# Three edits to a two-layer attention kernel: the last image's fourth row tile behind the flag, the projection's first tiles by head pairs, and one addition between normed tiles

## Chip, cores and metric

One NeuronCore of one Trainium2 chip runs the whole kernel. The time is device microseconds of one execution; the runs agree within about 0.3%. Engines are named as in the profile: PE is TensorE (PEld are its weight loads), DVE is VectorE, ACT is ScalarE, POOL is GpSimd, SP is SyncE, which issues DMAs.

## The reference, cut to what matters

The input is 8 images of 1024 tokens (32 x 32) with 384 channels, in float32. Each image goes through two layers.

```python
def _gn(v, G=32, eps=1e-5): ...            # group norm, 32 groups of 12 channels
def _ln_t(v, eps=1e-5): ...                # layer norm over the channels

# layer 0: 6 heads of 64, biases by row and column position
qkv = x.reshape(b, hw, c) @ qkv_w + qkv_b
attn = einsum('bqd,bkd->bqk', q * SCALE, k) + rel_h + rel_w
out = einsum('bqk,bkd->bqd', softmax(attn), v)          # per head
x = x + (out.reshape(b, h, w, c) @ proj_w + proj_b)     # qkv from _gn(x)
# layer 1: one causal head over 1024 tokens, width 384
t = x.reshape(b, 1024, 384)
q, k, v = (_ln_t(t) @ W for W in (Wq, Wk, Wv))
t = t + softmax(where(causal, q @ k.T * scale, -inf)) @ v
# layer 1: two linear maps with signs of weights (384 -> 1536 -> 384), each followed by
# a scaling by the largest absolute value of the image; only images 0 to 4 are not zero here
t = t + bitlinear(gelu(bitlinear(_ln_t(t), W1, b1)), W2, b2)
```

The groups of the last part are single images (8 // 5 = 1), so that images 5, 6 and 7 get nothing from it.

## The kernel before

**Order of images.** Images are done one after the other in `ORDER`: 5, 0, 1, 2, 3, 4, 6, 7. `AFTER` maps each image to the next one; image 7 alone isn't in it. While one image is in layer 1, work for the next one's group norm is slipped in.

**Order of the work.** The program is written in order, and the scheduler of the tile framework places each instruction in its engine's queue, by priority and by its own model of when operands are ready. Two helpers tie it down: `tc.issue_after(ins)` and `behind_of(ins)` put what is issued inside them behind the instruction named. `last_matmul`, `last_product`, `last_ended` and `last_normed` hold the last such instruction of a chain. Engines meet through semaphores. All eight PSUM banks are one pool of 128 x 512 float32 tiles (`o_tile`), so that a new product waits until a bank has been read out.

**Layer 0** (`layer0`, `attend0_fast`). Tokens are halves of 512, heads are pairs of two (`p` = 0, 1, 2). For each pair and half, eight key tiles give scores (L905, L909), ScalarE takes the exponent (L916), the values are summed with them (L931), and VectorE adds up the exponents (L921, L923). `oT` holds the result with channels on partitions, as three blocks of 128 channels, one for each pair. The pair and half before is divided late: its sums go through a small product `den` (L965), a reciprocal (L972), a widening (L979, L980), and a multiplication. For the last pair, half 0 is multiplied by L1013 and half 1 by L1016, both on VectorE. Then the output projection is made for eight tiles of 128 tokens (`project`, L520): three products over the pairs, accumulated in a bank. Tiles 0 to 3 lie in half 0 and are asked for at L1018 in the order tile by tile; tiles 4 to 7 come by `begin`. `more(j)` (L1024) adds a tile to the residual `xt`.

**Layer 1, projections** (`attention1`). `normed` takes mean and variance of four tiles and gives the normed tiles (L490). `turn_normed` transposes each of them (three products with the identity into one bank `pt`, L427; ScalarE copies it out, L428). Queries and values are made with a fast multiplication of 3 x 3 blocks: 15 products instead of 18 (`ProductSet`, in the order `PROD_ORDER`) are summed in six banks A to F. Partial sums are copied out by ScalarE (`keep`, L639) and combined by GpSimd (L659). When a bank's last product and its second operand are there, `final` subtracts or adds the two on VectorE (L1098 for queries, L1106 for values), which ends the bank's use. The tenth product makes the operand `n3`, which completes bank E's second operand `m7`; before, `of_q.final` is None in that step, so that E's addition comes with the next call, behind all four normed tiles of the second half:

```python
of_q.final = None
of_q.run(1)
with behind_of(last_ended[0]), behind_of(of_q.last_copy):
    tiles, _ = next(norm)
    tiles = list(tiles)
last_ended[0] = last_normed[0]
of_q.run(4, put_queries(0))
```

**Layer 1, attention** (`attend1_fast`). `scores(c)` makes the transposed scores of key tile `c`, and `values(j)` sums the products of row tile `j` over its `j + 1` key tiles. The values carry a 385th column of ones, so that the sum of a row stands beside it. VectorE copies that sum (L1205), takes its reciprocal (L1206), and adds the scaled row to `xt` (L1207). `values(c - 2)` follows `scores(c)`; tiles 6 and 7 come last. For images 0 to 4 the feed-forward part follows.

**The end.** `check` (L561, L562) notes the sums and reciprocals in `seen`. After all images, `judge` compares them with limits (L282), reduces them to `worst` (L284, L285), adds that over partitions by a product (L287), and writes `flag` (L288). Every engine loads the flag (L1497) and branches (L1498): if it isn't zero, the whole work is done once more in a safer form, the general path. Here it is zero. The outputs are stored by pairs of row tiles (L1482); for image 7 SyncE does that, in the order (0, 1), (2, 3), (4, 5), (6, 7).

Of the kernel before, what the change touches and what calls it, by code (L numbers as in the profile page):

```python
# [19 lines left out]
P = 128  # L20
B, H, W, C = 8, 32, 32, 384
T = H * W
NJ = T // P
# [68 lines left out]
def conv_attn_hybrid(  # L92
# [182 lines left out]
    seen = const.tile([P, 2, N_SEEN], F32, name="seen")  # L275
    flag = const.tile([1, 1], I32, name="flag")

    def judge(pools):

        bad = pools.page("bad")[:, : 2 * N_SEEN].rearrange("p (i n) -> p i n", i=2)  # L280
        for i, most in enumerate((SUM_MAX, RSUM_MAX)):
            nc.vector.tensor_scalar(bad[:, i, :], seen[:, i, :], most, -1.0, ALU.is_lt, ALU.mult)  # L282
        worst = const.tile([P, 1], F32, name="worst")
        nc.vector.tensor_reduce(worst, bad, AX.XY, ALU.max)  # L284
        nc.vector.tensor_scalar_add(worst, worst, 1.0)  # L285
        ps = pools.o_tile("bad")
        nc.tensor.matmul(ps[0:1, 0:1], worst, ones[:, 0:1], start=True, stop=True)  # L287
        nc.vector.tensor_copy(flag, ps[0:1, 0:1])  # L288

# [125 lines left out]
    def stages(pools):  # L417
# [471 lines left out]
        def attend0_fast(residual, b, q, k, r, v, later):  # L889
# [125 lines left out]
            rb = widened(p, half, reciprocals(*waiting))  # L1015
            nc.vector.tensor_tensor(oT[:, p, t], av, rb, ALU.mult)  # L1016
            with behind_last():
                begun = {j: project(wproj_sb, slice(0, C), oT, j, f"pj_{b}_{j}") for j in range(4)}  # L1018

            def begin(j):  # L1020
                begun[j] = project(wproj_sb, slice(0, C), oT, j, f"pj_{b}_{j}")
# [56 lines left out]
        def attention1(xt, more, b, between, start):  # L1078
# [36 lines left out]
            if pools.fast:  # L1115
                begin, more = more
                for j in range(4):
                    more(j)
                *_, (tiles, _) = normed(xt, 0, f"1_{b}")
                tiles = list(tiles)  # L1120
                begin(4)
                norm = normed(xt, 1, f"1_{b}")
                with behind_of(last_normed[0]):
                    more(4)
                    next(norm)
                last_ended[0] = last_normed[0]
                begin(5)
                turn_normed(xT, 0, tiles)
                begin(6)
                begin(7)  # L1130
                forms = forms_of(0)
                with behind_of(last_ended[0]):
                    for j in range(5, NJ):
                        more(j)
                        next(norm)
                    next(norm)
                last_ended[0] = last_normed[0]
                of_q, of_v = products(0, forms)
                of_q.run(9, put_queries(0))
                of_q.final = None  # L1140
                of_q.run(1)
                with behind_of(last_ended[0]), behind_of(of_q.last_copy):
                    tiles, _ = next(norm)
                    tiles = list(tiles)
                last_ended[0] = last_normed[0]
                of_q.run(4, put_queries(0))
                of_v.run(1)
                of_q.run(1)
                with behind_of(last_product[0]):
                    turn_normed(xT, 1, tiles)  # L1150
                last_product[0] = last_transpose[0]
                forms = forms_of(1)
                of_v0, (of_q, of_v) = of_v, products(1, forms)
                of_v0.run(13, put_values(0))
                of_q.run(1)
                of_v0.run(1)
                of_q.run(13, put_queries(1))
                of_v.run(1)
                of_q.run(1)
                queries_ended[0] = last_ended[0]  # L1160
                of_v.run(14, put_values(1))
            else:
                layer_norm_T(xt, xT, 0, f"1_{b}")
                layer_norm_T(xt, xT, 1, f"1_{b}")
                for m in range(NC):
                    queries(0, m)
                    queries(1, m)
                for j in range(NJ):
                    values(j)
# [6 lines left out]
        def attend1_fast(xt, b, q, xT, v, other, start):  # L1176
# [5 lines left out]
            def scores(c):  # L1182
# [15 lines left out]
                    nc.scalar.activation(pr[:, at : at + 512 - lo], sc[:, lo:], AF.Exp)  # L1198
                return pr

            def values(j):
                av = pools.o_tile(f"av1_{b}_{j}")
                for c in range(j + 1):
                    nc.tensor.matmul(av[:, : C + 1], prs[c][:, ts(j - c, P)], v[:, c, :], start=(c == 0), stop=(c == j))  # L1204
                nc.vector.tensor_copy(tot[:, j : j + 1], av[:, C : C + 1])  # L1205
                nc.vector.reciprocal(rt[:, j : j + 1], tot[:, j : j + 1])  # L1206
                nc.vector.scalar_tensor_tensor(  # L1207
                    xt[:, j, :], av[:, :C], rt[:, j : j + 1], xt[:, j, :], ALU.mult, ALU.add
                )

            prs, masked = [], [None]
            for c in range(NJ):
# [10 lines left out]
                signs.clear()  # L1223
            start()
            values(NJ - 2)
            values(NJ - 1)
            check(tot, rt, b * PER_IMAGE + PER_IMAGE - 1)

        def attend1_general(xt, b, q, xT, v, other, start):
            next(other, None)  # L1230
            mask = pools.work.tile([P, P], F32, tag="mask", name=f"mask_{b}")
            make_causal_mask(nc, mask, mask_val=MASKED)

            def scores(j):
                n = (j + 1) * P
                sc = []
                for half in range((n + 511) // 512):
                    sc.append(pools.o_tile(f"s1_{b}_{j}_{half}"))
                    w = min(512, n - half * 512)
                    for k in range(NC):  # L1240
                        nc.tensor.matmul(
                            sc[half][:, :w], q[:, j // 4, k, ts(j % 4, P)], xT[:, half, k, :w],
                            start=(k == 0), stop=(k == NC - 1),
                        )
                own = sc[j // 4][:, ts(j % 4, P)]
                nc.vector.tensor_tensor(own, own, mask, ALU.add)
                tot = pools.small.tile([P, 1], F32, tag="tot1", name=f"tot1_{b}_{j}")
                return softmax_numerator(sc, n, tot, f"1_{b}_{j}"), tot

            def values(j, got):  # L1250
                pr, tot = got
                prT = transpose_probs(pr, j + 1, f"prT1_{b}_{j}")
                av = pools.o_tile(f"av1_{b}_{j}")
                for c in range(j + 1):
                    nc.tensor.matmul(av[:, :C], prT[:, c, :], v[:, c, :C], start=(c == 0), stop=(c == j))
                rt = pools.small.tile([P, 1], F32, tag="rt1", name=f"rt1_{b}_{j}")
                nc.vector.reciprocal(rt, tot)
                nc.vector.scalar_tensor_tensor(xt[:, j, :], av[:, :C], rt, xt[:, j, :], ALU.mult, ALU.add)

            pipelined(range(NJ), scores, values)  # L1260
# [137 lines left out]
        def run(pools):  # L1398
# [49 lines left out]
            for b in ORDER:  # L1448
# [37 lines left out]
                if b < B_FFN:  # L1486
                    unfinished.append(finish)
                else:
                    finish(*range(NJ))

        run(pools)

    with ExitStack() as scope:
        pools = Pools(scope, tc, "f")
        stages(pools)
        judge(pools)
    failed = nc.values_load(flag[0:1, 0:1], min_val=0, max_val=P)  # L1497
    with tc.If(failed > 0), ExitStack() as scope:  # L1498
        stages(Pools(scope, tc, "g"))
# [38 lines left out]
```

## Time and profile before

| | us |
|---|---|
| median of 3 runs | 2274.53 |
| lowest and highest | 2273.84, 2279.3 |
| profiled execution, its own time | 2274.38 |
| its span, first to last instruction | 2272.6 |
| PE busy | 2258.0 (99%) |
| DVE busy | 1627.1 (72%) |
| ACT busy | 1208.3 (53%) |
| POOL busy | 527.9 (23%) |
| mean granted TensorE clock | 0.999 |

The span is what the trace covers; the execution's own time is 1.8 us longer. A line of the page or of the groups gives a source line, an engine and operation, what is written from what, how often, the busy time and mean ns. In a list of waits, a line names the waiting engine and line, what it waited for, the total us, how often, and the longest. A timeline line gives the start, the length, and in brackets the idle time before it. A "q" behind an engine's name means its queue: register, branch, semaphore and DMA-issuing instructions. Matmuls overlap in the array, and their ends are modelled.

### The profile page before, as it was taken

The numbers are of one execution on the slowest core, as the hardware profiler recorded it, in microseconds if no ns is written. First come the engines' busy times: TensorE is split into PE (matmuls) and PEld (weight loads), VectorE is DVE, ScalarE is ACT, GpSimd is POOL, SyncE is SP. The second block draws the span as 40 slices with busy tenths as digits, with TensorE's granted clock in tenths as the row PEclk, the third lists the DMA queues.
The fourth block names the chain that finished last, engine by engine and source line by source line (L and its number), as shares of the span: only waits on it lengthen the run. The fifth ranks groups of instructions, "written<-read, shape, count | busy, mean of one in ns | idle before, by whom it ended". The sixth has DMA issues, their size and how long they took to land.

```text
span 2272.6 us, 30133 instructions
## 1 busy us (share of the span) xinstructions
PE 2258.0 (99%) x10589; PEld 1384.9 (61%) x10589; DVE 1627.1 (72%) x2746; ACT 1208.3 (53%) x2181; POOL 527.9 (23%) x696
## 2 busy tenths in 40 slices
PE   9999999999999999999999999999999999999998
PEld 4547554768546677547685475874577754755474
DVE  6888588876888548886468884578854788737872
ACT  4644266337664356644467543766444766326641
POOL 7513231230131301313102312013040131221320
PEclk9999999999999999999999999999999999999999
DMA  6520562130730205510318203064002362017100
GB/s 192 154 84 28 164 135 68 51 144 29 156 98 29 84 28 131 127 53 1 112 47 182 55 29 111 28 145 109 30 21 91 88 156 68 1 51 163 42 1 30
DMA packets 182047, 188.48 MB, mean 83 GB/s; under 512 B 138763, under 2 KB 151488, under 8 KB 179072
## 3 DMA queue, kind: packets, MB, share of 16 engines
q1 hardware_dynamic: 163680, 115.80, 20.9%
q0 software_dynamic: 17376, 69.30, 9.6%
q8 instruction: 86, 1.41, 0.3%
q10 hardware_dynamic: 832, 1.38, 0.2%
q14 instruction: 73, 0.60, 0.1%
HBM read 84.52 MB, written 51.56 MB: 60 GB/s over the span
## 4 chain that ended last, share of the span: by engine, by line
PE 98%; DVE 1%; issue 0%; DVEq 0%
PE f_s L905 15%; PE f_av L931 15%; PE f_s L1189 8%; PE f_av L1204 8%; PE f_y L1364 7%; PE f_y L1314 7%; PE f_qk L574 6%; PE f_pj L520 5%; PE f_s L909 4%; PE f_pr_A L574 4%; PE f_pr_B L574 3%; PE f_rel L574 2%; PE f_pr_1v_A L574 2%; PE f_pr_1q_A L574 2%; PE f_pr_1v_B L574 2%; PE f_pr_1q_B L574 1%
## 5 line engine op out<-in xcount | busy, mean ns | idle before, releaser
L916 ACT ACTIVATE f_pr<-f_s 128x512 f32<-128x512 f32 x768 | 412.5, 595 | 42.2 <-PE f_s L909 38.3
L905 PE MATMUL f_s<-f_q,f_k 64*128 64x512 f32 x1536 | 399.2, 595 | 0.0
L923 DVE TENSOR_TENSOR f_sum<-f_sum,f_pr 128x1024 f32<-128x1024 f32 x288 | 365.3, 1268 | 25.8
L931 PE MATMUL f_av<-f_pr,f_v 128*64 128x512 f32 x1536 | 340.2, 595 | 0.0
L909 PE MATMUL f_s<-f_r,unit 64*128 64x512 f32 x768 | 308.0, 793 | 0.0
L931 PEld LDWEIGHTS f_av<-f_pr,f_v 128*64 128x64 f32 x1536 | 106.0, 137 | 218.2 <-issue 191.9
L905 PEld LDWEIGHTS f_s<-f_q,f_k 64*128 64x128 f32 x1536 | 146.0, 186 | 124.0 <-issue 66.5
L1189 PE MATMUL f_s<-f_q,f_lnT 128*128 128x512 f32 (+3 forms) x576 | 198.2, 488 | 0.0
L1204 PE MATMUL f_av<-f_v,f_pr 128*128 128x385 f32 x576 | 195.3, 486 | 0.0
L796 POOL DMA_DIRECT2D f_r<-f_far x192 | 101.9, 533 | 388.0 <-DVE f_far L790 172.5
L1198 ACT ACTIVATE f_pr<-f_s 128x512 f32<-128x512 f32 (+3 forms) x96 | 47.0, 490 | 205.0 <-DVE f_s L1194 162.1
L1204 PEld LDWEIGHTS f_av<-f_v,f_pr 128*128 128x128 f32 x576 | 108.2, 190 | 77.3 <-issue 11.5
L1189 PEld LDWEIGHTS f_s<-f_q,f_lnT 128*128 128x128 f32 x576 | 100.8, 190 | 70.3 <-issue 46.9
L1325 DVE TENSOR_REDUCE am<-f_h 128x1 f32<-128x1024 f32 (+2 forms) x80 | 71.6, 946 | 95.6 <-ACT f_h L1318 95.6
L1318 ACT ACTIVATE f_h<-f_y,biases 128x256 f32<-128x256 f32 x240 | 100.6, 470 | 67.0 <-PE f_y L1314 67.0
L520 PE MATMUL f_pj<-wproj_sb,f_oT 128*128 128x384 f32 x384 | 129.4, 490 | 1.4 <-DVE f_oT L1013 1.4
L909 PEld LDWEIGHTS f_s<-f_r,unit 64*128 64x128 f32 x768 | 75.2, 187 | 89.7 <-issue 89.2
L574 PE MATMUL f_qk<-f_gnT,wq_sb 128*128 128x512 f32 x288 | 127.9, 595 | 0.0
L1364 PE MATMUL f_y<-f_w2a,f_hilo 128*128 128x384 f32 x640 | 127.2, 341 | 0.0
L1003 ACT COPY f_oT<-f_av 128x512 f32<-128x512 f32 x40 | 23.4, 586 | 190.2 <-PE f_av L931 190.2
L921 DVE TENSOR_TENSOR f_sum<-f_pr,f_pr 128x1024 f32<-128x1024 f32 x48 | 62.8, 1309 | 80.8 <-ACT f_pr L916 80.8
L1364 PEld LDWEIGHTS f_y<-f_w2a,f_hilo 128*128 128x128 f32 x640 | 112.6, 188 | 3.8 <-DVE f_hilo L1342 1.4
(282 smaller groups left out, 4058.9 us busy)
## 6 DMA issues: line engine op xcount, KB each, us to landing
f_far<-f_far SPq DMA_DIRECT2D x48, 512.0 KB, 4.8
f_r<-f_far SPq DMA_DIRECT2D x192, 128.0 KB, 3.1
f_r<-f_far POOLq DMA_DIRECT2D x192, 128.0 KB, 4.5
f_far<-f_far SPq DMA_DIRECT2D x192, 64.0 KB, 4.6
f_x<-in_x SPq DMA_DIRECT2D x32, 384.0 KB, 4.4
f_gnT<-in_xT SPq DMA_DIRECT2D x21, 512.0 KB, 4.9
f_w1a<-w1s POOLq DMA_DIRECT2D x5, 1536.0 KB, 6.6
f_w2a<-w2s POOLq DMA_DIRECT2D x5, 1536.0 KB, 7.3
```

The source lines that it names most:

```text
L520: nc.tensor.matmul(ps[:, :C], xT[:, k, ts(j, P)], w[:, k, cols], start=(k == 0), stop=(k == NC - 1))
L574: last_product[0] = nc.tensor.matmul(*args, **kw).ins
L796: put = (nc.gpsimd if i else nc.sync).dma_start(out=r(part, p).bitcast(F32).rearrange("(m i) t -> i m t", i=4)[2 * i + d], in_=pages[i][ts ...
L905: nc.tensor.matmul(sc[par], k[rows[par], p, ts(c, P)], q[rows[par], p, ts(half, 512)], start=True, stop=False)
L909: last_matmul[0] = nc.tensor.matmul(sc[par], unit[rows[par], c // 2 % 2].rearrange("i h w -> i (h w)"), r(2 * (c // 4) + c % 2, p)[rows[pa ...
L916: last_exp[0] = nc.scalar.activation(pr[:, ts(par, 512)], sc[par], AF.Exp).ins
L923: adds.append(nc.vector.tensor_tensor(total, total, pr, ALU.add).ins)
L931: last_matmul[0] = nc.tensor.matmul(av[ts(par, HD), :], v[:, c, ts(2 * p + par, HD)], pr[:, ts(par, 512)], start=(c == 0), stop=(c == NJ - 1),
L1189: last_score[0] = nc.tensor.matmul(sc[:, lo:], xT[:, c // 4, k, ts(c % 4, P)], q[:, half, k, lo:], start=(k == 0), stop=(k == NC - 1),).ins
L1204: nc.tensor.matmul(av[:, : C + 1], prs[c][:, ts(j - c, P)], v[:, c, :], start=(c == 0), stop=(c == j))
L1314: nc.tensor.matmul(ps, w1k[i // 2][:, ts(m, P)], xs[i % 2][:, half, i // 2, :], start=(i == 0), stop=(i == 2 * NC - 1))
L1364: nc.tensor.matmul(ps[:, :C], h, w, start=(i == 0), stop=(i == len(products) - 1))
```

## The change

1. Tail. In image 7 (`held` is 3), `values(3)` only makes the row's sum, by products with a column of ones, and its reciprocal. Tile 7's addition to `xt` is put off. Then `values_and_flag` makes tile 3's products over key tiles 0 to 2; `judge_sums` (the part of `judge` on VectorE) comes before tile 7's addition; the flag's product is put behind those of tile 3 so far, and the last product of tile 3 behind that. The stores of image 7 end with the pair (2, 3).
2. Projection. Tiles 0 and 1 do their products over pairs 0 and 1 first, then those over pair 2, then tiles 2 and 3 follow; each is tied behind the one before. This holds for all images.
3. Addition. In the projections of layer 1, two normed tiles are made, then bank E's addition, then the other two. This holds for all images.

A loop in `attend1_general` belongs to the general path.

```diff
--- before.py
+++ after.py
@@ -275,17 +275,21 @@
     seen = const.tile([P, 2, N_SEEN], F32, name="seen")
     flag = const.tile([1, 1], I32, name="flag")
 
-    def judge(pools):
+    def judge_sums(pools):
 
         bad = pools.page("bad")[:, : 2 * N_SEEN].rearrange("p (i n) -> p i n", i=2)
         for i, most in enumerate((SUM_MAX, RSUM_MAX)):
             nc.vector.tensor_scalar(bad[:, i, :], seen[:, i, :], most, -1.0, ALU.is_lt, ALU.mult)
         worst = const.tile([P, 1], F32, name="worst")
         nc.vector.tensor_reduce(worst, bad, AX.XY, ALU.max)
-        nc.vector.tensor_scalar_add(worst, worst, 1.0)
+        made = nc.vector.tensor_scalar_add(worst, worst, 1.0).ins
+        return worst, made
+
+    def judge(pools, worst):
         ps = pools.o_tile("bad")
-        nc.tensor.matmul(ps[0:1, 0:1], worst, ones[:, 0:1], start=True, stop=True)
+        made = nc.tensor.matmul(ps[0:1, 0:1], worst, ones[:, 0:1], start=True, stop=True).ins
         nc.vector.tensor_copy(flag, ps[0:1, 0:1])
+        return made
 
 
 
@@ -1015,7 +1019,13 @@
             rb = widened(p, half, reciprocals(*waiting))
             nc.vector.tensor_tensor(oT[:, p, t], av, rb, ALU.mult)
             with behind_last():
-                begun = {j: project(wproj_sb, slice(0, C), oT, j, f"pj_{b}_{j}") for j in range(4)}
+                begun = {j: pools.o_tile(f"pj_{b}_{j}")[:, :C] for j in range(4)}
+                for j, ks in ((0, (0, 1)), (1, (0, 1)), (0, (2,)), (1, (2,)), (2, (0, 1, 2)), (3, (0, 1, 2))):
+                    for i in ks:
+                        with tc.issue_after(last_matmul[0]):
+                            last_matmul[0] = nc.tensor.matmul(
+                                begun[j], oT[:, i, ts(j, P)], wproj_sb[:, i, :], start=(i == 0), stop=(i == NC - 1)
+                            ).ins
 
             def begin(j):
                 begun[j] = project(wproj_sb, slice(0, C), oT, j, f"pj_{b}_{j}")
@@ -1140,10 +1150,15 @@
                 of_q.final = None
                 of_q.run(1)
                 with behind_of(last_ended[0]), behind_of(of_q.last_copy):
-                    tiles, _ = next(norm)
-                    tiles = list(tiles)
+                    made, _ = next(norm)
+                    tiles = list(itertools.islice(made, 2))
                 last_ended[0] = last_normed[0]
-                of_q.run(4, put_queries(0))
+                of_q.final = put_queries(0)
+                of_q.finish()
+                with behind_of(last_ended[0]):
+                    tiles += made
+                last_ended[0] = last_normed[0]
+                of_q.run(4)
                 of_v.run(1)
                 of_q.run(1)
                 with behind_of(last_product[0]):
@@ -1198,15 +1213,45 @@
                     nc.scalar.activation(pr[:, at : at + 512 - lo], sc[:, lo:], AF.Exp)
                 return pr
 
+            def products(av, j, cs, what):
+                for c in cs:
+                    made = nc.tensor.matmul(av, prs[c][:, ts(j - c, P)], what(c), start=(c == 0), stop=(c == j)).ins
+                return made
+
+            def total(j, av):
+                nc.vector.tensor_copy(tot[:, j : j + 1], av)
+                nc.vector.reciprocal(rt[:, j : j + 1], tot[:, j : j + 1])
+
+            def add(j, av):
+                return nc.vector.scalar_tensor_tensor(
+                    xt[:, j, :], av[:, :C], rt[:, j : j + 1], xt[:, j, :], ALU.mult, ALU.add
+                ).ins
+
             def values(j):
                 av = pools.o_tile(f"av1_{b}_{j}")
-                for c in range(j + 1):
-                    nc.tensor.matmul(av[:, : C + 1], prs[c][:, ts(j - c, P)], v[:, c, :], start=(c == 0), stop=(c == j))
-                nc.vector.tensor_copy(tot[:, j : j + 1], av[:, C : C + 1])
-                nc.vector.reciprocal(rt[:, j : j + 1], tot[:, j : j + 1])
-                nc.vector.scalar_tensor_tensor(
-                    xt[:, j, :], av[:, :C], rt[:, j : j + 1], xt[:, j, :], ALU.mult, ALU.add
-                )
+                if j == held:
+                    products(av[:, :1], j, range(j + 1), lambda c: ones[:, 0:1])
+                    total(j, av[:, :1])
+                    return
+                products(av[:, : C + 1], j, range(j + 1), lambda c: v[:, c, :])
+                total(j, av[:, C : C + 1])
+                if held is not None and j == NJ - 1:
+                    return av
+                add(j, av)
+
+            def values_and_flag(j, av7):
+                av = pools.o_tile(f"av1_{b}_{j}")
+                last = products(av[:, :C], j, range(j), lambda c: v[:, c, :C])
+                worst, made = judge_sums(pools)
+                with tc.issue_after(made):
+                    add(NJ - 1, av7)
+                with tc.issue_after(last):
+                    last = judge(pools, worst)
+                with tc.issue_after(last):
+                    products(av[:, :C], j, (j,), lambda c: v[:, c, :C])
+                add(j, av)
+
+            held = None if b in AFTER else 3
 
             prs, masked = [], [None]
             for c in range(NJ):
@@ -1223,11 +1268,14 @@
                 signs.clear()
             start()
             values(NJ - 2)
-            values(NJ - 1)
+            av7 = values(NJ - 1)
             check(tot, rt, b * PER_IMAGE + PER_IMAGE - 1)
+            if held is not None:
+                values_and_flag(held, av7)
 
         def attend1_general(xt, b, q, xT, v, other, start):
-            next(other, None)
+            for _ in other:
+                pass
             mask = pools.work.tile([P, P], F32, tag="mask", name=f"mask_{b}")
             make_causal_mask(nc, mask, mask_val=MASKED)
 
@@ -1486,14 +1534,13 @@
                 if b < B_FFN:
                     unfinished.append(finish)
                 else:
-                    finish(*range(NJ))
+                    finish(*(range(NJ) if b in AFTER else (0, 1, 4, 5, 6, 7, 2, 3)))
 
         run(pools)
 
     with ExitStack() as scope:
         pools = Pools(scope, tc, "f")
         stages(pools)
-        judge(pools)
     failed = nc.values_load(flag[0:1, 0:1], min_val=0, max_val=P)
     with tc.If(failed > 0), ExitStack() as scope:
         stages(Pools(scope, tc, "g"))
```

## The prediction

> **What bounds the kernel now.** I read the page first, then the waits of TensorE, then the timeline at three places, taking the starts of single instructions from narrow windows.
>
> ```profile
> PE   9999999999999999999999999999999999999998
> PEclk9999999999999999999999999999999999999999
> ```
>
> TensorE is busy in every slice at full clock, except for the last one. Only idle TensorE time can be won, so the waits are listed by engine.
>
> ```profile
> PE f_bad L287 <- DVE worst L285: 1.9, 1, 1.9
> ...
> PE f_pj L520 <- DVE f_oT L1013: 1.4, 8, 0.2
> ```
> ```profile
> PEld f_pj L520 <- DVE f_oT L1013: 6.3, 8, 0.8
> ...
> PEld f_pt L427 <- DVE f_q L1098: 3.0, 8, 0.4
> ```
>
> (Total us, times, longest.) The three edits touch exactly these waits: the projection (8 times), the transposes of the second half (8 times), the flag (once). The totals can't be used as they stand: the weight loads count time in which matmuls still ran, and the matmuls' modelled ends hide part of a hole. I take the distances between starts of matmuls instead: 0.3225 us for 384 columns and 0.109 for 128, each a half of one fp32 product (every product is two instructions).
>
> ```profile
> 2192.45 2.25 DVE L490 TENSOR_SCALAR f_xn<-f_x,lmv,lrs 128x384 f32<-128x384 f32 x4
> 2193.52 0.96 POOL L659 TENSOR_TENSOR f_u_1q<-f_u_1q 128x256 f32<-128x256 f32 x1 [0.62 <-DVE f_xn L490]
> 2194.62 0.41 DVE L1098 TENSOR_TENSOR f_q<-f_pr_1q_E,f_u_1q 128x256 f32<-128x256 f32 x1
> 2194.96 0.41 DVE L1098 TENSOR_TENSOR f_q<-f_pr_1q_F,f_u_1q 128x256 f32<-128x256 f32 x1
> 2195.09 0.64 PEld L427 LDWEIGHTS f_pt<-ident,f_xn 128*128 128x128 f32 x6 [0.38 <-DVE f_q L1098]
> 2195.29 0.41 DVE L1098 TENSOR_TENSOR f_q<-f_pr_1q_C,f_u_1q 128x256 f32<-128x256 f32 x1
> 2195.75 0.52 PEld L574 LDWEIGHTS f_pr_1v_B<-w1f,f_xf 128*128 128x128 f32 x4
> ```
>
> See that the second six transpose loads (2195.09) start when the final addition of bank E ends (2194.62 + 0.41), and that the next load, 1v_B at 2195.75, starts just as bank C's ends (2195.29 + 0.41). PSUM banks come free one by one behind VectorE.
>
> ```profile
> 2264.14 0.14 DVE L288 CAST flag<-f_bad 1x1 int32<-1x1 f32 x1 [0.28 <-PE f_bad L287]
> ```
> ```profile
> L1498 POOLq COMPARE_BRANCH  x1: 62/62/62, 2265.2 to 2265.2; - x1
> L1498 SPq COMPARE_BRANCH  x1: 50/50/50, 2265.5 to 2265.5; - x1
> L1498 POOLq INC_SWDGE_SEM  x1: 572/572/572, 2269.5 to 2269.5; - x1
> ```
>
> Every engine loads the flag at 2264.3, branches, and does its next instruction at 2268.9 to 2269.2. After that GpSimd's 1.6 us drain (2270.14 to 2271.75) ends last; SyncE had drained at 2270.87.
>
> **What the skill says.** "Perfetto Trace Analysis", summary of the profiler window: TensorE's ends are estimates; hence starts here. "SBUF — State Buffer", who interferes with whom: GpSimd and a VectorE operation in a two-port mode, or with two SBUF inputs, exclude each other on a shared port; whichever is first runs to its end. The trace agrees: the four L490 take 0.67, 0.47, 0.47, 0.89 us where 0.47 is the median; the first and last ran into a GpSimd subtraction and ended 0.215 us after it did. L1106 at 2202.45 (one input in PSUM) took 0.41 while GpSimd worked. "TensorE: Matmul & The Clock Gate", LDWEIGHTS: the load costs its columns, so 128 columns some 107 ns whatever N; the one-column products of L452 step by 0.111 us. "Runtime: NRT & Kernel Launch", instruction fetch mechanics: a taken branch refetches instructions; here 3.7 us on SyncE, 3.9 on GpSimd.
>
> **Edit 2, projection by head pairs.** In the last image the starts are 2169.872, 2170.299, 2170.621, 2170.944, then 2171.600, 2172.026. The fifth (pair 2 of tile 0) waits for L1013, which ends at 2171.545. The hole is 0.656 - 0.323 = 0.333, and the first load after a stop isn't hidden: 0.426 - 0.3225 = 0.104. Sum 0.437; the eight images show 0.43 to 0.45. Now four more halves (tile 1, pairs 0 and 1) come first, and pair 2 is reached at 2171.267 + 4 x 0.3225 = 2172.56, 0.96 us after it is ready. The stall goes, with nothing added. What is late next: tile 0 ends at 2173.37 rather than 2172.51, so the first addition L1024 starts near 2173.39 instead of 2173.35; VectorE takes that 0.04 up in its 0.46 us of idleness before the third. The third and fourth wait for TensorE and come 0.44 earlier, and so do norms and transposes behind them. **8 x 0.437 = 3.5 us gained.** Bounds 3.0 to 3.6.
>
> **Edit 3, bank E's addition between normed tiles.** From the first transpose (time 0): the starts step by 0.109, save 0.414 before the seventh, 0.164 after it, 0.159 after 1v_B's first. The hole is 0.305 + 0.055 + 0.05 = 0.41 per image, 3.3 in eight. Not all of it goes, because the fourth transposed tile takes bank F and 1v_B takes C, and their additions stay behind all four normed tiles. Before: L490 starts at -1.68, -1.09, -0.70, -0.31; E +0.49, F +0.83, C +1.16. GpSimd subtracts at -1.96 (this makes E's second operand, ready at -1.23) and at -0.61, where the third L490 held it up and it then held up the fourth.
>
> After: E starts where the third stood, -0.70, waits for nothing, takes 0.41 and, reading one SBUF input, leaves GpSimd alone. GpSimd starts at -0.61 and takes its usual 0.726, to +0.12. The third L490 is issued at -0.70 + 0.334 = -0.37, is shut out, and ends at 0.12 + 0.215 = 0.335. The fourth ends at 0.335 - 0.08 + 0.47 = 0.72, F starts at 0.65 (before 0.83), C ends at 1.39 (before 1.57). So 1v_B starts 0.18 earlier, not 0.41. **8 x 0.18 = 1.5 us.** Bounds: 0 if F keeps its time, 3.3 if GpSimd stays out of the way.
>
> **Edit 1, the tail**, last image only.
> - Added: tile 3's sums by ones, 4 products = 8 halves of N = 1, each with a 128-column load. L452 shows 0.027 for the first (loaded ahead), 0.111 for each further one, and 0.084 for the load exposed behind: 0.027 + 7 x 0.111 + 0.084 = 0.89 us of TensorE. That a column less is streamed later is nothing.
> - Moved: tile 3's 8 halves (8 x 0.3235 = 2.59) go behind tile 7. TensorE's stream ended at 2261.86; tile 7 now ends at 2261.86 + 0.89 - 2.59 = 2260.16, and VectorE starts its sums 0.2 later (2262.06 before), at 2260.36. Without L1207 (0.53 in the chain) L285 ends at 2260.36 + 1.80 - 0.53 = 2261.63. TensorE does six halves until 2262.10, so the flag's product doesn't wait: margin 0.4 us. That is the cover; without it TensorE stands still.
> - The flag product costs 0.05 and an exposed load 0.08; flag written near 2262.5 rather than 2264.29, **1.8 earlier**. The last two halves end at 2262.9, the final addition is at 2263.13 to 2263.75.
> - Queues: the DMA of tiles 2 and 3 is issued on SyncE at 2263.77 (before, the last one at 2263.10), takes 0.37, and SyncE's load of the flag stands behind it: 2264.19 against 2264.31. SyncE gains only 0.12; its DMA lands (2.4 us) well before 2269. The pair 6 and 7 goes near 2262.2.
> - What ends last: GpSimd's end moves from 2271.75 to about 2270.0, SyncE's drain from 2270.87 to 2270.75 and takes over. **1.0 us gained.** Bounds: 0.1 if GpSimd's drain awaits SyncE, 1.8 if only the flag counts.
>
> The other edit in the general path changes nothing that is run.
>
> **Sum.** 3.5 + 1.5 + 1.0 = 6.0 us. The profiled execution took 2274.38 (span 2272.59 and 1.79 around it), so 2268.4; the median of the runs is 0.15 higher, so **2268.5 us**.
>
> **Rivals.**
> - *F and C stay where they are* (VectorE loses as much to GpSimd as before). For: 1v_B's load leaves only 0.05 us behind C's end. Against: L490 is the only stretched operation there. 3.5 + 0 + 1.0: 2270.0. Chance 0.22, with a tail of 0.1 included.
> - *All holes close* (GpSimd out of the way, the tail limited by the flag): 3.5 + 3.3 + 1.8 = 8.6: 2265.9. Against: the order on SyncE. Chance 0.12.
> - *Edit 2 doesn't do what it says*, the wait being for the whole of oT and not the half: the stall moves to tile 0's start. Against: two products already run ahead of L1013. Gain 2.5: 2272.0. Chance 0.05.
> - *Slower*: E's addition is held by GpSimd in the middle of the normed tiles. GpSimd's subtractions are ordered behind VectorE's last step (L658), and the second one starts at -0.61, just after the second L490 ends (-0.62); the profile even names that as its wait. If the first one came there too, both would run from -0.61 to +0.12 and +0.85, E would start at 0.87, the L490 behind it at 1.20 and 1.59, F at 1.98, and C would end at 2.72, 1.15 later than now: 8 x 1.15 = 9.2 lost against 4.5 gained, 2279.2. It decides once E starts over 0.74 later than -0.70 (the 0.18 of edit 3 gone, then (3.5 + 1.0) / 8 = 0.56 more). Against: the first subtraction (2192.17) was done 0.53 before E's place at -0.70, and nothing that it waits for is moved. Chance 0.04.
>
> **Numbers.** Forecast 0.57, by itself 2267.4 to 2269.6. The range, 2265.8 to 2271.0, takes in the first two rivals. A measurement of this kernel tells about 0.3% (6.8 us) from no change; the bound lies at 2267.7. All of the full case and a fifth to a quarter of the forecast's own spread lie below: faster 0.27, same 0.69, slower 0.04.
>
> **What would show it.** Right: steps of 0.3225 from the second to the last projection start; E's L1098 between two pairs of L490, GpSimd's second subtraction back at 0.73, the third L490 near 0.70; pt's seventh start at 0.11 after the sixth with a smaller hole before the tenth; the flag written some 1.2 us before the last addition ends, SyncE's branch last. Wrong: a stop at pair 2, E's start late, or a stop of TensorE before L287.

## The result, and the profile after

The changed kernel takes **2267.53 us** (median of 7 runs, 2267.45 to 2271.02) against 2274.53 us (median of 7 runs) for the kernel before. The ratio is 0.997 with a 95% interval of 0.9958 to 0.9981: 7.0 us, 0.31%, are gone. The forecast was 2268.5; its three terms were 3.5 + 1.5 + 1.0 = 6.0 us.

The profiled execution is the longest of the seven, 2271.02 us (span 2269.2), because TensorE falls 3.54 us behind in the first image (last section); the parts of the trace that follow are read as differences of starts after it. 2271.02 - 3.54 = 2267.5, the median, so the runs near the median, by their times, don't have this stop.

The slices look as before, so nothing is to be learned from them but that TensorE still sets the time:

```profile
PE   9999999999999999999999999999999999999998
PEclk9999999999999999999999999999999999999999
```

The waits of TensorE in the changed kernel (engine and line, what it waited for, total us, times, longest):

```profile
PE f_s L909 <- DVE f_v L829: 2.4, 1, 2.4
PE f_zeros L403 <- DVE f_zeros L401: 1.5, 1, 1.5
```
```profile
PEld f_pt L431 <- DVE f_q L1108: 1.7, 8, 0.2
...
PEld f_bad L290 <- DVE f_x L1226: 0.5, 1, 0.5
```

All lines on f_pj are gone, and so is the 1.9 us of the flag's product on PE: what is left there is the stop of this one execution and waits at the start. The transposes still wait 8 times, 1.7 us in all instead of 3.0. The last line is read with care: the weight load of the flag's product waits for tile 7's addition (L1226), which ends at 2260.81, but for most of that time matmuls ran. TensorE's turn would have come at 2260.75 (the start of the half before it, 2260.43, and 0.32); the product starts at 2260.84, so 0.09 is lost.

**The projection** of the last image on TensorE (start, length, how many), in the kernel before:

```profile
2169.87 1.56 PE L520 MATMUL f_pj<-wproj_sb,f_oT 128*128 128x384 f32 x4
2171.60 1.88 PE L520 MATMUL f_pj<-wproj_sb,f_oT 128*128 128x384 f32 x5 [0.17 <-DVE f_oT L1013]
```

and in the changed kernel, with VectorE below:

```profile
2169.13 4.78 PE L1026 MATMUL f_pj<-wproj_sb,f_oT 128*128 128x384 f32 x14
```
```profile
2170.11 0.69 DVE L1017 TENSOR_TENSOR f_oT<-f_oT,f_wide 128x512 f32<-128x512 f32 x1
...
2172.00 0.69 DVE L1020 TENSOR_TENSOR f_oT<-f_av,f_wide 128x512 f32<-128x512 f32 x1
2172.66 0.56 DVE L1034 TENSOR_TENSOR f_x<-f_pj,f_x 128x384 f32<-128x384 f32 x1
```

One unbroken group of matmuls runs across L1017's end at 2170.80; before, TensorE stood still for that end. From the start of the projection to the first transpose behind it, the eight images gain 0.43 to 0.45 each: **3.51 us**.

**Bank E's addition** in the last image, VectorE, GpSimd and TensorE's loads:

```profile
2191.27 1.06 DVE L494 TENSOR_SCALAR f_xn<-f_x,lmv,lrs 128x384 f32<-128x384 f32 x2
2192.25 0.41 DVE L1108 TENSOR_TENSOR f_q<-f_pr_1q_E,f_u_1q 128x256 f32<-128x256 f32 x1
2192.58 1.10 DVE L494 TENSOR_SCALAR f_xn<-f_x,lmv,lrs 128x384 f32<-128x384 f32 x2
2193.60 0.41 DVE L1108 TENSOR_TENSOR f_q<-f_pr_1q_F,f_u_1q 128x256 f32<-128x256 f32 x1
```
```profile
2192.34 0.73 POOL L663 TENSOR_TENSOR f_u_1q<-f_u_1q 128x256 f32<-128x256 f32 x1 [0.62 <-DVE f_xn L494]
```
```profile
2192.74 1.12 PEld L431 LDWEIGHTS f_pt<-ident,f_xn 128*128 128x128 f32 x9
2194.07 0.31 PEld L431 LDWEIGHTS f_pt<-ident,f_xn 128*128 128x128 f32 x3 [0.21 <-DVE f_q L1108]
2194.40 0.52 PEld L578 LDWEIGHTS f_pr_1v_B<-w1f,f_xf 128*128 128x128 f32 x4
```

E stands between the pairs and takes its plain 0.41. GpSimd starts at 2192.34, takes its plain 0.73 and ends at 2193.07, in the middle of the second pair; that pair takes 1.10, where an unhindered pair takes 0.86 (an experiment below shows one): its first tile is shut out. So nine loads, not six, now run in one group, and the stop has moved from the seventh to the tenth, where it waits for F (2193.60 + 0.41 = 2194.01). Per image 0.17 to 0.19, in eight **1.39 us**.

**The tail**, all engines in order of start:

```profile
2259.01 0.16 DVE L1222 COPY tot<-f_av 128x1 f32<-128x1 f32 x1 [4.18 <-PE f_av L1218]
...
2260.13 0.15 DVE L285 TENSOR_SCALAR worst<-worst 128x1 f32<-128x1 f32 x1
2260.20 0.61 DVE L1226 SCALAR_TENSOR_TENSOR f_x<-f_av,rt,f_x 128x384 f32<-128x384 f32 x1
...
2260.84 0.19 PE L290 MATMUL f_bad<-ones,worst 128*1 128x1 f32 x2
...
2261.06 0.15 DVE L291 CAST flag<-f_bad 1x1 int32<-1x1 f32 x1 [0.26 <-PE f_bad L290]
2261.91 0.62 DVE L1226 SCALAR_TENSOR_TENSOR f_x<-f_av,rt,f_x 128x384 f32<-128x384 f32 x1 [0.70 <-PE f_av L1218]
```

The judgement's last step (L285) ends at 2260.28, 0.56 before the product starts; the flag is written at 2261.21, the last addition ends at 2262.53, 1.3 later. The tail gains **2.05 us** from 1v_B of the last image to the end of the span, twice what was forecast. The sequencers' instructions show where (count: ns min/median/max, first and last start in us). SyncE in the kernel before, where it branches at 2265.47 and goes on at 2269.21:

```profile
L1497 SPq TENSOR_LOAD <-flag x1: 763/763/763, 2264.3 to 2264.3; - x1
```
```profile
L1498 SPq EVENT_SEMAPHORE  x8: 17/17/17, 2269.2 to 2269.8; - x8
```

In the changed kernel:

```profile
L1544 POOLq TENSOR_LOAD <-flag x1: 496/496/496, 2261.2 to 2261.2; - x1
...
L1544 SPq TENSOR_LOAD <-flag x1: 493/493/493, 2263.0 to 2263.0; - x1
```
```profile
L1545 SPq EVENT_SEMAPHORE  x8: 17/17/17, 2266.9 to 2267.5; - x8
...
L1545 POOLq COMPARE_BRANCH  x1: 62/62/62, 2261.8 to 2261.8; - x1
...
L1545 SPq COMPARE_BRANCH  x1: 50/50/50, 2263.9 to 2263.9; - x1
```

SyncE's branch comes last, 2.05 us after GpSimd's, as its load stands behind the store of tiles 2 and 3. But it branches at 2263.86 and goes on at 2266.95, in 3.08 us instead of 3.74, and the load took 0.49 instead of 0.76. SyncE's drain at 2268.36 then ends the kernel; GpSimd's was over at 2267.42. The sum by the trace is 3.51 + 1.39 + 2.05 = 6.95, the 7.0 of the medians.

### The profile page after: what moved, and what is told of

It reads as the page before. It is cut to its first block, busy times and chain, and to the rows that moved or that the text cites. A ratio compares the mean times of both kernels' runs of the same rounds, so it can differ in the third digit from the quotient of the medians.

```text
span 2269.2 us, 30149 instructions
## 1 busy us (share of the span) xinstructions
PE 2257.0 (99%) x10597; PEld 1387.8 (61%) x10597; DVE 1633.2 (72%) x2746; ACT 1208.3 (53%) x2181; POOL 527.2 (23%) x696
## 4 chain that ended last, share of the span: by engine, by line
PE 99%; DVE 0%; DMA 0%; SPq 0%; issue 0%; ACT 0%
PE f_s L909 15%; PE f_av L935 15%; PE f_av L1218 8%; PE f_s L1204 8%; PE f_y L1412 7%; PE f_y L1362 7%; PE f_qk L578 6%; PE f_s L913 4%; PE f_pr_A L578 4%; PE f_pr_B L578 3%; PE f_pj L1026 3%; PE f_pj L524 3%; PE f_rel L578 2%; PE f_pr_1v_A L578 2%; PE f_pr_1q_A L578 2%; PE f_pr_1v_B L578 2%
## 5 line engine op out<-in xcount | busy, mean ns | idle before, releaser
L1218 PE MATMUL f_av<-f_v,f_pr 128*128 128x385 f32 (+1 forms) x576 | 195.4, 486 | 0.0
```

Of the source, the lines that this page charges most:

```text
L1218: made = nc.tensor.matmul(av, prs[c][:, ts(j - c, P)], what(c), start=(c == 0), stop=(c == j)).ins
```

## The experiments

### One edit at a time

The kernel before, with the hunk of the projection alone:

```
-                begun = {j: project(wproj_sb, slice(0, C), oT, j, f"pj_{b}_{j}") for j in range(4)}
+                begun = {j: pools.o_tile(f"pj_{b}_{j}")[:, :C] for j in range(4)}
+                for j, ks in ((0, (0, 1)), (1, (0, 1)), (0, (2,)), (1, (2,)), (2, (0, 1, 2)), (3, (0, 1, 2))):
...
```

> The kernel before with the projection's new order alone. If the gain is the sum of the holes that each edit closes: the stop at the fifth projection start goes in all eight images, 8 x 0.44 = 3.5 us, 2271.0 against 2274.5, and nothing else moves. If the stops only move on to a later place (the first additions of tile 0 and 1 coming late), the transposes behind would start less than 0.44 earlier in each image, and the time would stay above 2272.5.

Measured: 2271.08 us (15 runs) against 2274.63 for the kernel before (35 runs), ratio 0.9982 (0.9974 to 0.9989). By the trace the eight images gain 0.43 to 0.45, 3.51 in all. In its waits of TensorE's loads the line on f_pj is missing, and the others stand as they did in the kernel before:

```profile
PEld f_pt L427 <- DVE f_q L1104: 3.0, 8, 0.4
PEld f_bad L287 <- DVE worst L285: 2.5, 1, 2.5
```

So the stall went and came back nowhere: the first step of the forecast holds alone.

With the hunk of the additions alone:

```
-                    tiles, _ = next(norm)
-                    tiles = list(tiles)
+                    made, _ = next(norm)
+                    tiles = list(itertools.islice(made, 2))
...
-                of_q.run(4, put_queries(0))
+                of_q.final = put_queries(0)
+                of_q.finish()
+                with behind_of(last_ended[0]):
+                    tiles += made
+                last_ended[0] = last_normed[0]
+                of_q.run(4)
```

> The kernel before with the addition of bank E between the normed tiles alone. My theory: GpSimd's second subtraction shuts the third normed tile out, F and C come only 0.17 to 0.18 us earlier, so 8 x 0.175 = 1.4 us, 2273.1. Rival: the wait for bank E (0.41 us a time) is the whole loss and goes as a whole: 3.3 us, 2271.2. Second rival: nothing is won because the fourth normed tile is what is late: 2274.5.

Measured: 2273.49 us (13 runs) against 2274.63, ratio 0.9993 (0.9984 to 1.0001). The interval holds no change as well, so the times alone don't settle it; the trace does: counted from the first transpose of the second half, 1v_B comes 0.17 to 0.18 earlier in each image, 1.39 in all.

With the hunks of the tail alone (`judge` in two parts, tile 3 held, its sums by ones, the order of the stores):

```
-            values(NJ - 1)
+            av7 = values(NJ - 1)
             check(tot, rt, b * PER_IMAGE + PER_IMAGE - 1)
+            if held is not None:
+                values_and_flag(held, av7)
...
-                    finish(*range(NJ))
+                    finish(*(range(NJ) if b in AFTER else (0, 1, 4, 5, 6, 7, 2, 3)))
```

> The kernel before with the held row tile alone. By the recorded forecast SyncE's path gains 0.12 us and the end 1.0: 2273.5. By what the changed kernel's trace shows (SyncE's load of the flag 0.49 instead of 0.76 us and its refetch 3.1 instead of 3.7 us, since the other engines are no longer at the same step, and no wait for GpSimd): 2.0 to 2.1 us, 2272.5.

Measured: 2272.46 us (13 runs) against 2274.63, ratio 0.9993 (0.9985 to 1.0001; 10 runs lie between 2272.1 and 2273.7, 3 above 2275.6). Here too the interval holds no change. The difference of the medians is 2.2, and its trace has the tail of the changed kernel: from 1v_B to the end 2.19 less than before, with SyncE's load at 0.494 us and 2.96 from its branch to its next instruction. Why these are shorter, the expectation says and this run alone doesn't show; the experiments below bear on it. The three parts add up by their medians, 3.55 + 1.14 + 2.17 = 6.86, to within 0.3 of the 7.1 of all together against the same 2274.63.

### Two additions between the normed tiles

The stop left in edit 3 waits for F, which stands behind four normed tiles. Here F goes ahead of the third one too:

```
                 of_q.finish()
+                of_q.run(2)
                 with behind_of(last_ended[0]):
                     tiles += made
                 last_ended[0] = last_normed[0]
-                of_q.run(4)
+                of_q.run(2)
```

> The changed kernel with bank F's addition, too, before the third normed tile. If GpSimd's subtraction is what holds the third tile up, F fits into the time for which it is shut out anyway: the third and fourth tiles end as before, the stop before the tenth transpose (0.14 + 0.055 us) goes, C comes about where it is, 0.33 earlier by one addition less behind the fourth tile, and each image gains some 0.2 us: 1.4 to 1.9 us, 2265.7 to 2266.2. If VectorE's own rate is the limit, moving F only delays the third and fourth tiles by 0.33 us each: no gain or a loss of up to 1 us, 2267.5 to 2268.5.

Measured: 2265.30 us (5 runs, 2264.9 to 2265.74), ratio to the kernel before 0.9954 (0.9941 to 0.9968), 2.2 below the changed kernel. VectorE and TensorE's loads in the last image:

```profile
2186.93 0.41 DVE L1108 TENSOR_TENSOR f_q<-f_pr_1q_E,f_u_1q 128x256 f32<-128x256 f32 x1
2187.26 0.41 DVE L1108 TENSOR_TENSOR f_q<-f_pr_1q_F,f_u_1q 128x256 f32<-128x256 f32 x1
2187.59 0.86 DVE L494 TENSOR_SCALAR f_xn<-f_x,lmv,lrs 128x384 f32<-128x384 f32 x2
```
```profile
2187.41 1.45 PEld L431 LDWEIGHTS f_pt<-ident,f_xn 128*128 128x128 f32 x12
2188.83 0.52 PEld L578 LDWEIGHTS f_pr_1v_B<-w1f,f_xf 128*128 128x128 f32 x4
```

All twelve transposes go in one group. The second pair takes 0.86, not 1.10: while GpSimd subtracts (2187.02 to 2187.75), VectorE now has E and F to do, which read one operand from PSUM and aren't held up, and the third normed tile, issued at 2187.59, loses next to nothing. Counted from the first transpose of the second half, 1v_B comes 0.18 to 0.19 earlier per image than in the changed kernel (1.52 in all), 1v_C another 0.05 (0.39), and in two images the time from there to the next projection is 0.14 and 0.15 shorter (0.29): 2.20. The expectation of 1.4 to 1.9 had left the last two out.

### The store of tiles 2 and 3 on ScalarE's queue

```
-                        (nc.gpsimd if b in AFTER else nc.sync).dma_start(
+                        (nc.gpsimd if b in AFTER else nc.scalar if j == 2 else nc.sync).dma_start(
```

> The changed kernel with the store of tiles 2 and 3 of the last image issued by ScalarE instead of SyncE. SyncE's load of the flag no longer stands behind that store and comes at the flag, some 1.7 us earlier. If load and refetch are short only when the other engines aren't at the same step, SyncE's load is back at 0.76 us and its refetch at some 3.7, and the end comes about 0.8 us earlier: 2266.7. If they are short for another reason (0.49 and 3.1), it comes until GpSimd's drain is last, some 1.0 us earlier or more: 2266.5. If the store's landing or ScalarE's own end is last, nothing is won: 2267.5.

Measured: 2267.01 us (5 runs, 2266.49 to 2267.18), ratio 0.9965 (0.9952 to 0.9979): 0.5 below the changed kernel. SyncE, by its load and by its next instructions:

```profile
L1544 SPq TENSOR_LOAD <-flag x1: 495/495/495, 2257.6 to 2257.6; - x1
```
```profile
L1545 SPq EVENT_SEMAPHORE  x8: 17/17/17, 2261.4 to 2263.1; - x8
...
L1545 SPq COMPARE_BRANCH  x1: 50/50/50, 2258.5 to 2258.5; - x1
```

SyncE now branches with the others and is back at 2261.41, but its eight semaphore steps are spread over 1.7 us instead of 0.6: one of them waits until 2262.63 for the store, issued on ScalarE at 2258.93, to land 3.7 us later. So the queue was the bound of the changed kernel, and half a microsecond behind it lies the landing of the last store. In this kernel that store sets the end. The second case of the expectation held for the durations: SyncE branches 0.33 us behind GpSimd and 0.30 behind TensorE, and still its load is 0.495 and its way back 2.90. So branching along with two other engines doesn't make SyncE's way back long.

### Both together

The two diffs above in one kernel.

> Both at once: bank F's addition before the third normed tile, and the store of tiles 2 and 3 on ScalarE. The two lie in different places, so the gains should add: 2265.3 less what the store on ScalarE gains, 2264.4 if that is 0.9 us.

Measured: 2264.61 us (5 runs, 2264.47 to 2269.95), ratio 0.9959 (0.9945 to 0.9972); the interval is wide because two of the five are 3.7 and 5.3 longer. By the median the gains add, 2.2 + 0.5 and 0.2 more, to 2.9 below the changed kernel and 9.8 below the kernel before in the runs taken beside it (2274.38): the best version found.

### Tile 2 held instead of tile 3

The same tail with a smaller cover: tile 2's six halves go behind tile 7 instead of tile 3's eight.

```
-            held = None if b in AFTER else 3
+            held = None if b in AFTER else 2
```

> The changed kernel with row tile 2 held instead of 3: two one-column halves fewer (6 for 8), two halves fewer behind tile 7 (6 for 8). By the price of 0.111 us a one-column half, TensorE's stream is 0.22 us shorter; four halves, 1.29 us, still cover the judgement of the sums, which in the changed kernel took 1.27 us from tile 7's sum to the sums' verdict, so the flag's product waits at most 0.2 us. The end follows SyncE and the last store: 0 to 0.2 us earlier, 2267.3 to 2267.5. If the cover is too short, TensorE stops before the flag's product by 0.3 us or more and the gain is lost.

Measured: 2267.70 us (6 runs, 2267.25 to 2268.23), ratio 0.9968 (0.9956 to 0.998). TensorE stops ahead of the flag's product, 0.33 us from its turn (2257.95, the last half's start and 0.32) to the product's start (2258.28). The list counts less of it, as the modelled end of the last half lies later:

```profile
PE f_bad L290 <- DVE worst L285: 0.2, 1, 0.2
```

In the changed kernel TensorE's turn comes 0.47 us after L285 (2260.75 and 2260.28). From L285's end to the product it takes 0.15 here (L285 ends at 2258.13), so 0.32 is spare there. Two halves less take 0.65 away: a stop of 0.33, as measured, where the expectation allowed at most 0.2. The changed kernel loses 0.09 at this place, so 0.24 more is lost; two one-column halves fewer (2 x 0.11) pay nearly all of it back, and the time is about that of the changed kernel.

### The flag written behind the last addition

The flag's cast moves behind tile 3's last addition; the products stay where they are. All five engines then load, branch and go on almost together, as they did in the kernel before.

```
-        nc.vector.tensor_copy(flag, ps[0:1, 0:1])
-        return made
+        return made, lambda: nc.vector.tensor_copy(flag, ps[0:1, 0:1])
...
-                add(j, av)
+                with tc.issue_after(add(j, av)):
+                    put_flag()
```

> The changed kernel with the flag written behind tile 3's last addition instead of before it, so that all five engines come to the flag's load within about 0.3 us, as in the kernel before. SyncE is where it was, behind the last store. If it is the company that makes load and refetch long: SyncE's load back at 0.74 to 0.78 us and its refetch at 3.6 us or more, GpSimd's too; GpSimd drains last again, and the end comes 1.5 us later or more: 2269.0. If a late SyncE is all that counts: SyncE's load 0.49 and refetch 3.1 us, the end at most 0.4 us later, 2267.5 to 2267.9.

Measured: 2269.30 us (9 runs, 2268.99 to 2269.83), ratio 0.9976 (0.9966 to 0.9986), 1.8 above the changed kernel, though the matmuls are the same. The loads and the branches:

```profile
L1544 DVEq TENSOR_LOAD <-flag x1: 547/547/547, 2259.4 to 2259.4; - x1
...
L1544 SPq TENSOR_LOAD <-flag x1: 494/494/494, 2259.7 to 2259.7; - x1
```
```profile
L1545 SPq EVENT_SEMAPHORE  x8: 17/17/17, 2264.1 to 2264.6; - x8
L1545 POOLq EVENT_SEMAPHORE  x5: 17/43/43, 2264.0 to 2264.3; - x5
...
L1545 POOLq COMPARE_BRANCH  x1: 62/62/62, 2259.9 to 2259.9; - x1
L1545 PEldq COMPARE_BRANCH  x1: 4880/4880/4880, 2260.0 to 2260.0; - x1
...
L1545 SPq COMPARE_BRANCH  x1: 50/50/50, 2260.6 to 2260.6; - x1
...
L1545 POOLq INC_SWDGE_SEM  x1: 572/572/572, 2264.4 to 2264.4; - x1
```

SyncE branches at 2260.62 and goes on at 2264.05: 3.43 us; ScalarE needs 3.94, GpSimd 4.08, VectorE 4.14, TensorE 4.9. GpSimd is again the one that ends last (its drain at 2266.65, SyncE's at 2265.76). Counted from 1v_C, GpSimd's flag is 1.37 later and its way back 1.10 longer than in the changed kernel; its drain there had 0.95 to spare, which leaves the 1.5 by which this trace ends later. By this sum 0.4 would have been lost with the way back as it was, so the longer way back is the larger part of the loss, but a later flag is in it too.

Neither case of the expectation came as it stood: the ways back are longer, but the loads stay at 0.47 to 0.55 in company. What goes with long loads is a store. In the kernel before and in the versions with the projection or the addition alone, some 200 of the 272 packets of the last store are under way while each load runs, from its start to about its end, and all five loads take 0.74 to 0.78. In the versions with the new tail, the loads of 0.46 to 0.55 meet none, a few, or the last packets of a store (76 here, 93 for SyncE with tile 2 held). Left out are VectorE's loads of 0.82 to 1.08, which begin before its own last addition has ended. That the store slows the load is the likely reading; no run takes the store away.

## Why the prediction was right, and which term was too small

**Edit 2.** 3.5 forecast, 3.51 by the trace, 3.51 and a median 3.55 lower with this edit alone. The rival in which the wait is for the whole of oT is excluded by the unbroken group of matmuls.

**Edit 3.** 1.5 forecast, 1.39 by the trace, 1.39 alone. The reasoning, step by step, holds too: measured from the first transpose E starts at -0.70 (forecast -0.70), GpSimd ends at +0.13 (+0.12), the third normed tile at +0.34 (+0.335), the fourth at +0.73 (+0.72), F starts at +0.65 (+0.65) and C ends at 1.40 (1.39). In the Trainium skill, "SBUF — State Buffer", who interferes with whom, says that whichever of the two starts first gets the shared port for its whole instruction; here that is the third normed tile at 0.71 us instead of 0.47. The experiment with two additions turns the argument round: with work of one SBUF operand there, nothing is shut out, and the rest of the hole closes. The rival "F and C stay" is excluded by F at +0.65 (it was at +0.83), "all holes close" by the hole before the tenth transpose, and "slower" by E's start at -0.70.

**Edit 1.** Here the mechanism was right and the size was off. Right: the ones cost 0.89 (0.81 for the products, 0.08 for the exposed load), the flag's product doesn't wait for the judgement (only 0.09 for tile 7's addition), SyncE's branch comes last and its drain takes over from GpSimd's. Too small: **"SyncE gains only 0.12"**, and with it "SyncE's drain from 2270.87 to 2270.75", which left 1.0 us of gain. Taken against TensorE, which is 1.35 us ahead at 1v_B of the last image, SyncE's drain comes 1.15 earlier, not 0.12. Its load starts no earlier (+0.02, forecast -0.12), and the rest lies behind it: the load is 0.27 shorter (0.493 for 0.763), the way back from the branch 0.66 shorter (3.08 for 3.74), and a wait of 0.24 for GpSimd's semaphore instruction is gone, since GpSimd is now ahead. 0.27 + 0.66 + 0.24 - 0.02 = 1.15. The forecast carried all three over from the kernel before as fixed durations. They aren't: the experiment with the late flag, in which the engines branch nearly together again, ends 1.8 later (1.5 by its trace), and GpSimd's way back is 1.10 longer there. GpSimd's own durations fell as well in the changed kernel (load 0.50 for 0.78, way back 2.98 for 3.95). Had only the flag moved for it, 1.73 us, its drain would still have ended 0.3 behind SyncE's new one. Before, the end hung on GpSimd's drain 0.88 later than SyncE's; 0.88 + 1.15 = 2.03, the gain in the tail to within 0.02.

What makes the way back long or short is not shown. In the Trainium skill, "Runtime: NRT & Kernel Launch", instruction fetch mechanics, says that a taken branch can force a transfer of the target page, and the trace agrees: between the branches and the way back, the DMA records of the kernel before hold one transfer of 16 KB and four of 8 KB in queues of the kind "instruction", from 2266.04 to 2267.52. They aren't the whole of the way back: the first begins 0.93 us after the first branch, and the engines go on at 2268.89 to 2269.21. That such fetches hold each other up fits most of the ten profiles and not all (last section), and stores may play a part: with the late flag and with tile 2 held, the first such transfer begins 1.57 and 1.65 us after the first branch, about when the packets of a store end, against 0.92 to 0.93 in the three profiles in which the packets end within 0.1 us of that branch. No run takes the stores away.

A smaller miss: "the flag product costs 0.05 and an exposed load 0.08". It took about 0.31: 0.09 ahead of it (the wait for tile 7's addition), 0.12 itself and 0.10 for the exposed load behind it, 0.2 more than forecast. It is felt at the end: counted against TensorE at 1v_B, the last addition ends 0.13 later than forecast (2263.88 for 2263.75), and the store and SyncE's load stand behind it, so that the load gains nothing instead of 0.12.

The forecast's total is 1.0 above the median: 1.05 too little for the tail, 0.1 too much for edit 3. That it came this near rests on the first two terms; the tail was half of what was measured.

## What to carry to other kernels

Where a VectorE step loses to GpSimd on their shared port, change the order: put steps with one operand in PSUM into the time in which GpSimd works (bank F's addition there took 0.41 and held nothing up). At the end of a program follow each engine by itself from its last load to its drain, with the DMA queue's store ahead of it, and don't take a branch's cost over from a version in which the engines branch at other times (SyncE's was 3.74 us before and 3.08 after). When a wait on the path goes, look for the next thing behind it by moving one queue's instruction: here it was a store's landing, 0.5 us behind.

## What the runs showed that was not expected

**VectorE can be shut out for many GpSimd instructions in a row.** The stop of 3.54 us in the profiled execution, 2.43 of it in one wait of TensorE, begins with one subtraction of VectorE in the first image, while GpSimd makes weight forms back to back; VectorE, GpSimd and TensorE:

```profile
63.51 6.18 DVE L663 TENSOR_TENSOR f_u<-f_u 128x512 f32<-128x512 f32 x1 [0.74 <-ACT f_u L643]
```
```profile
63.26 0.45 POOL L197 TENSOR_TENSOR w1f<-w1f,f_raw 128x128 f32<-128x128 f32 x1
...
68.69 1.31 POOL L197 TENSOR_TENSOR w1f<-w1f,f_raw 128x128 f32<-128x128 f32 x2
```
```profile
70.47 0.69 PE L909 MATMUL f_s<-f_q,f_k 64*128 64x512 f32 x1 [2.43 <-DVE f_v L829]
```

In the kernel before the same subtraction, at 63.52, took 0.88: it got in between two of GpSimd's instructions. Here it got in when fourteen more had started and ended, near 69.1, in a pause of GpSimd (69.13 to 69.21), and GpSimd's own next instruction is the stretched one; three additions (L829) and then TensorE waited for it. The same 6.17 us stands in the profile of the version with both edits, which took 2269.95 where its median is 2264.61. In seven of the ten profiles no TENSOR_TENSOR of VectorE takes over 2.5 us, so it comes and goes from execution to execution; the two profiled executions with this stop lie 3.5 and 5.3 us above the medians of their kernels. The profile with both edits has another of 6.76 us, and the one with two additions one of 7.03, and TensorE waits for neither. That such stops make the other long runs too, those without a profile, is likely and not shown.

**The way back from a taken branch** took 2.7 us on ScalarE, 3.0 on GpSimd, 3.1 on SyncE, 3.85 on TensorE and 4.0 on VectorE in the changed kernel, 3.7 to 4.0 on all five in the kernel before, 3.4 to 4.9 with the late flag. Over all ten profiles, ScalarE, GpSimd and SyncE need 3.4 to 4.2 where all five engines branch within 0.8 us (the kernel before, the projection alone, the addition alone, the late flag), and 2.6 to 3.3 elsewhere, with one exception: with tile 2 held, ScalarE, GpSimd and TensorE branch within 0.1 us of each other as in the changed kernel, and ScalarE and GpSimd need 3.5. VectorE (3.5 to 4.3) and TensorE (3.5 to 4.9) show no such order.
